# A cross-attention kernel: a new hand-written order of all engines and transfers

## The chip, the cores and the metric

The kernel runs on one core of a Trainium2 chip. The metric is the time of one execution on the device, in microseconds, and smaller is better. The time before is a median of three runs. One more execution was recorded by the profiler, and all rows of the trace come from that one.

## The reference

The layer is a cross-attention with two short sets of keys that share one set of queries. The batch is 2, a sequence has 2048 tokens of 640 channels, there are 20 heads of 32, and each set has 77 keys made from a context of 1024 channels. Everything is float32.

```python
q = split_heads(x @ Wq.T)                                   # (2, 20, 2048, 32)
k, v = split_heads(text @ Wk.T), split_heads(text @ Wv.T)   # 77 keys
k_ip, v_ip = split_heads(ip @ Wk_ip.T), split_heads(ip @ Wv_ip.T)
out = merge_heads(softmax(q k.T / sqrt(32)) v)
out += merge_heads(softmax(q k_ip.T / sqrt(32)) v_ip)
result = out @ Wo.T + bo + x
```

## The kernel before

All matrices lie with the contracted dimension first. A group of four heads fills the 128 partitions, so there are five groups of heads and two batches: ten pairs, q = 0 to 9. The tokens of a pair are taken in two halves of 1024, which gives twenty units, u = 0 to 19, and each half is two blocks of 512 tokens.

The body of the kernel is one long string, SCHEDULE. It is split into words, and `emit` turns each word into instructions. The framework adds the waits between engines that the data need, and each engine and the queue of SyncE (SP) run their own instructions strictly in the order of the string. The order of the words is therefore the order of each engine, and a word that waits holds up all later words of its engine. These are the words:

- `q.u.h@bank` (`queries`, L199): TensorE's query product of one block, ten instructions. `cq.u.h` is ScalarE's copy of it out of its bank.
- `k.c.t`, `v.c.t` (`project_kv`, L140): keys and values of a group of heads for one set, sixteen instructions each. `ck` and `cv` are their copies by ScalarE. `SQ.c` (L150) is VectorE's transposition of the values, and `VS.q.half` (`spread_v`, L156) spreads one half of them by eight small transfers of 20 KB.
- `Rs.u@half` (`scores`, L231): the scores of group s of unit u; groups 0 and 1 hold three tiles of 128 tokens (24 instructions), group 2 holds two (16). They fill four of the eight banks.
- `K` (ScalarE's copy of scores, L243), `M` (VectorE's maximum, L279 or L282), `S` (GpSimd's subtraction, L293), `E` (exponential, L299 or L267), `D` (VectorE's sum, L304), `I` (reciprocal, L309), `N` (GpSimd's normalisation, L314), `T` (VectorE's transposition, L321): the softmax of one group.
- `A.q@half` (`attend`, L330): attention of a pair, 160 instructions. `CA.q` is its copy.
- `m`, `G`, `W`, `o` and their copies `cm`, `co`: the output product of batch 0, as seven products per block (L488, L498) on sums that GpSimd makes. `p`, `z`, `F`, `V`, `X`, `Y`, `yz`: the output product of batch 1, with 33 products (L469, L846) on sums of weights (`V`) and of tokens (`X`); the last letter, `p` or `d`, says whether GpSimd or VectorE makes them. `Y` adds a product to an output and sends the output when it is complete.
- Transfers on SP: `LX.u.h` a block of tokens of batch 1 (1280 KB, `load_block`, L184), `LQ.q` query weights (320 KB, L190), `LK.n` key or value weights (512 KB, `load_w`, L130), `LO` the output weights (1600 KB, L162), `SF.i.part` residual rows (256 KB), `SS.i.part` finished rows (256 KB).

A load waits until the last reader of its buffer is done. Three buffers hold query weights, four hold key and value weights, and three hold the tokens of batch 1, in turn:

```python
def place_of(u, h):
    _, b, _, sub = step_of(u)
    return late.index((u, h)) % XROOM if b else sub * NH + h

def load_w(n):
    src, c = wlist[n]
    w = wslots[n % len(wslots)]
    nc.sync.dma_start(out=w, in_=src[:, ts(c, P)].rearrange("(k p) o -> p k o", p=P))

def load_wq(q):
    c = q % NC
    nc.sync.dma_start(
        out=wqs[q % 3], in_=WqT[:, ts(c, P)].rearrange("(k p) o -> p k o", p=P)
    )
```

So LX.10.1 waits for q.10.0, LQ.6 for q.7.1, and LX.14.1 for q.14.0.

Three sets choose the form of a group's softmax. A group in none of them takes the words K, M, S, E, D, I, N, T, with one exponential for the whole group. A group in BIASED has no S: its exponential is row by row, with the maximum as a bias. A group in DIRECT has no K either; its maximum and its exponential read the scores' banks. A group in SUMMED has no D: the exponential adds up its sums. Twenty-one groups of sixty were row by row.

Of the kernel before, what the change touches and what calls it, by code (L numbers as in the profile page):

```python
# [20 lines left out]
def kernel(  # L21
# [43 lines left out]
        (11, 0), (12, 0), (13, 0), (13, 2), (14, 0), (14, 2), (15, 1), (15, 2), (16, 2), (18, 1),  # L65
    }
    BIASED = {
        (3, 2), (4, 0), (5, 2), (6, 2), (8, 2), (9, 2), (10, 2), (11, 2), (12, 2), (18, 2), (19, 2),
    }
    SUMMED = {  # L70
        (10, 2), (12, 0), (12, 2), (13, 0), (13, 2), (14, 0), (15, 1), (16, 2), (18, 1), (18, 2), (19, 2),
# [480 lines left out]
    for t in range(2):  # L552
# [336 lines left out]
```

## Time and profile before

| | |
|---|---|
| median of three runs | 499.93 us (498.37 to 500.46) |
| the profiled execution | 503.08 us, span 501.3 us |
| mean granted clock of TensorE | 0.997 |
| TensorE (PE) busy | 492.2 us, 98% |
| VectorE (DVE), ScalarE (ACT), GpSimd (POOL) busy | 410.7, 306.8, 376.5 us |
| moved | 69.38 MB, mean 138 GB/s |
| TensorE's products | 4114 |

The span runs from the first to the last instruction of the program; the execution's time has 1.8 us more around it. In the rows, PE is TensorE's products and PEld its weight loads, which run beside the products. A row of the chain has its start in us, its length in us, and what ran. In the timelines, a bracket at the end has the idle time before the instruction and what released it. A row of the waits has the total in us, the count and the longest. A row of the groups has the busy time in us and the mean of one in ns. In the table of stretches, a row has the length, the busy time and the count of each engine, then TensorE's granted clock, the share of the DMA engines and GB/s. In the DMA view, q1 is the transfers that the kernel issues and q8 is a queue of instructions: packets, MB, and share of the engines' time.

### The profile page before, as it was taken

What the parts mean: (1) busy time and instruction counts of PE and PEld (TensorE: products, weight loads), DVE (VectorE), ACT (ScalarE), POOL (GpSimd) and SP (SyncE); (2) the same over time, 40 slices, a digit from 0 to 9 for tenths busy, and PEclk for the clock granted to TensorE, in tenths of its full rate; (3) what the DMA queues carried; (4) which work ended last, traced back from release to release, by engine and by line L of the source; (5) the groups of instructions that cost most, each with busy time, mean ns of one, the idle gap of its engine ahead of it and who ended that gap; (6) DMA issues with size and microseconds to landing.
All of it is one profiled execution on the core that took longest, in us unless ns stands there. A gap on an engine that the chain in (4) does not pass through costs nothing.

```text
span 501.3 us, 10439 instructions
## 1 busy us (share of the span) xinstructions
PE 492.2 (98%) x4114; PEld 290.7 (58%) x4114; DVE 410.7 (82%) x409; ACT 306.8 (61%) x970; POOL 376.5 (75%) x166
## 2 busy tenths in 40 slices
PE   9999999999999989999999999999999999999997
PEld 5665757567557547446646655665655685444442
DVE  0069989989999986978996888678799889998875
ACT  1175768798786866757999877485677955100000
POOL 0079998779898895968876748665889889799850
PEclk9999999999999998999999999999999999999999
DMA  8975403243044490748416337628442203320125
GB/s 264 356 209 151 133 3 100 54 119 84 23 112 150 150 288 19 248 133 330 134 54 229 94 119 274 222 87 264 144 158 90 86 1 106 127 84 1 43 101 192
DMA packets 67473, 69.38 MB, mean 138 GB/s; under 512 B 5472, under 2 KB 47200, under 8 KB 67424
## 3 DMA queue, kind: packets, MB, share of 16 engines
q1 hardware_dynamic: 66704, 68.00, 43.0%
q8 instruction: 32, 0.52, 0.4%
q10 hardware_dynamic: 720, 0.72, 0.4%
q14 instruction: 17, 0.14, 0.1%
HBM read 54.94 MB, written 10.49 MB: 131 GB/s over the span
## 4 chain that ended last, share of the span: by engine, by line
PE 90%; DMA 6%; SPq 2%; issue 1%; DVE 0%; ACT 0%
PE bank L199 30%; PE bank L846 11%; PE bank L488 10%; PE bank L231 10%; PE bank L330 10%; PE bank L140 9%; PE bank L469 7%; PE bank L498 3%; DMA x<-in_x_dram 2%; DMA aT<-in_L_xattn_Wk_ip_dram 2%; DMA wq<-in_L_xattn_Wq_dram 1%; DMA wo_ct<-in_L_xattn_Wo_dram 1%; SPq L156 1%; SPq L532 1%; SPq L130 0%
## 5 line engine op out<-in xcount | busy, mean ns | idle before, releaser
L314 POOL TENSOR_TENSOR pb<-pb,rden 128x1848 f32<-128x1848 f32 (+1 forms) x60 | 176.0, 2942 | 39.2 <-DVE rden L309 35.1
L199 PE MATMUL bank<-x,wq 128*128 128x512 f32 x400 | 180.0, 600 | 0.1
L293 POOL TENSOR_TENSOR pb<-pb,mx 128x1848 f32<-128x1848 f32 (+1 forms) x39 | 121.7, 3129 | 60.4 <-DVE mx L279 55.3
L199 PEld LDWEIGHTS bank<-x,wq 128*128 128x128 f32 x400 | 74.5, 191 | 85.9 <-issue 82.3
L321 DVE STREAM_TRANSPOSE pb<-pb 128x1920 f32<-128x1920 f32 (+1 forms) x60 | 115.8, 1934 | 6.3 <-POOL pb L314 5.9
L279 DVE TENSOR_REDUCE mx<-pb 128x24 f32<-128x1848 f32 (+1 forms) x50 | 91.4, 1843 | 31.6 <-ACT pb L243 31.5
L243 ACT COPY pb<-bank 128x462 f32<-128x462 f32 (+1 forms) x200 | 85.3, 540 | 42.2 <-PE bank L231 41.8
L304 DVE TENSOR_REDUCE den<-pb 128x24 f32<-128x1848 f32 (+1 forms) x49 | 91.5, 1878 | 15.6 <-ACT pb L299 11.9
L299 ACT ACTIVATE pb<-pb 128x1848 f32<-128x1848 f32 (+1 forms) x39 | 65.4, 1680 | 17.2 <-POOL pb L293 17.0
L267 ACT ACTIVATE pb<-bank,mx 128x77 f32<-128x77 f32 x208 | 59.1, 390 | 12.3 <-DVE mx L282 12.2
L231 PEld LDWEIGHTS bank<-kT,qT 32*128 32x128 f32 x1280 | 45.8, 184 | 29.7 <-issue 20.3
L231 PE MATMUL bank<-kT,qT 32*128 32x154 f32 x1280 | 57.0, 306 | 3.3 <-issue 2.6
L330 PE MATMUL bank<-pb,v 32*32 32x512 f32 x1600 | 55.2, 597 | 0.0
L267 ACT ACTIVATE pb<-pb,mx 128x77 f32<-128x77 f32 x184 | 52.7, 357 | 1.1 <-DVE mx L279 0.8
L140 PE MATMUL bank<-wo_ct,aT 128*128 128x154 f32 x320 | 46.9, 302 | 0.2 <-DMA aT<-in_L_xattn_Wk_ip_dram 0.2
L140 PEld LDWEIGHTS bank<-wo_ct,aT 128*128 128x128 f32 x320 | 44.4, 194 | 3.4 <-issue 2.8
L330 PEld LDWEIGHTS bank<-pb,v 32*32 32x32 f32 x1600 | 30.4, 103 | 21.7 <-issue 9.6
L267 ACT ACTIVATION_READ_ACCUMULATOR pb<-bank,mx 128x1 f32 x152 | 40.2, 273 | 0.0
L469 PE MATMUL bank<-aT,wo_ct 128*128 128x512 f32 x80 | 36.4, 596 | 0.0
L209 ACT ACTIVATE qT<-bank 128x512 f32<-128x512 f32 x40 | 24.3, 613 | 19.4 <-PE bank L199 19.3
L488 PE MATMUL bank<-aT,wo_ct 128*128 128x256 f32 x128 | 32.5, 386 | 0.6 <-DMA wo_ct<-in_L_xattn_Wo_dram 0.6
L488 PEld LDWEIGHTS bank<-aT,wo_ct 128*128 128x128 f32 x128 | 23.6, 190 | 8.3 <-issue 4.0
(75 smaller groups left out, 435.8 us busy)
## 6 DMA issues: line engine op xcount, KB each, us to landing
x<-in_x_dram SPq DMA_DIRECT2D x20, 1280.0 KB, 7.1
out_dram<-acc SPq DMA_DIRECT2D x20, 256.0 KB, 2.3
x<-in_x_dram SPq DMA_DIRECT2D x18, 256.0 KB, 5.4
acc<-in_x_dram SPq DMA_DIRECT2D x16, 256.0 KB, 3.7
out_dram<-x SPq DMA_DIRECT2D x15, 256.0 KB, 2.1
v<-vS SPq DMA_DIRECT2D x160, 20.0 KB, 2.0
wq<-in_L_xattn_Wq_dram SPq DMA_DIRECT2D x9, 320.0 KB, 4.7
aT<-in_L_xattn_Wk_dram SPq DMA_DIRECT2D x5, 512.0 KB, 5.6
```

Of the source, the lines that this page charges most:

```text
L140: nc.tensor.matmul(keys_in(out), loaded[n][:, k, :], cT[:, k, :, t, :], start=(k == 0), stop=(k == NCC - 1))
L199: nc.tensor.matmul(pq, wqs[q % 3][:, k, :], xs[place_of(u, h)][:, k, :], start=(k == 0), stop=(k == NC - 1),)
L231: nc.tensor.matmul(ps[g][:, ts(t, 2 * L)], qTs[(u, h)][g * D : (g + 1) * D, ts(st, P)], kT[g * D : (g + 1) * D, c, b].rearrange("p t l -> ...
L243: nc.scalar.copy(keys_of(u, s)[:, :, g], ps[g][:, : n * 2 * L].rearrange("p (n l) -> p n l", n=n))
L267: nc.scalar.activation(row, row if ps is None else rows_in(ps[g], n)[:, t, x], AF.Exp, bias=maxs[(u, s)][:, *one], accum_out=None if den i ...
L279: nc.vector.tensor_reduce(mx, rows_of(u, s), AX.X, ALU.max, negate=negate)
L293: nc.gpsimd.tensor_tensor(rows_of(u, s), rows_of(u, s), maxs[(u, s)].unsqueeze(3).to_broadcast([P, n, 2, L]), ALU.subtract)
L304: nc.vector.tensor_reduce(den_of(u, s), rows_of(u, s), AX.X, ALU.add)
L314: nc.gpsimd.tensor_tensor(rows_of(u, s), rows_of(u, s), rdens[(u, s)].unsqueeze(3).to_broadcast([P, n, 2, L]), ALU.mult)
L321: nc.vector.transpose(p, p)
L330: nc.tensor.matmul(pa[r][g * D : (g + 1) * D, :], v4s[q % 2][rows, g, k, :], zones[rows, :, g, k, :], start=(k == 0), stop=(k == NK - 1),)
L488: nc.tensor.matmul(part, w_of[m][:, kp, op], t_of(m, b, i)[:, kp], start=(op == kp == 0 and m in (1, 2, 5)), stop=(op == 1 and kp == 1 and ...
```

## The change

Only the three sets and the string change. The same words stand in it, except for those of seven groups whose form changes and for twenty sums V and X that change their engine, ten each way. TensorE's order is nearly the same up to A.9: a few neighbours are exchanged. Behind A.9 its products come in another order. The transfers on SP are in a new order throughout, and the words of the other engines are exchanged with neighbours in many places. Twenty groups are row by row.

```diff
     DIRECT = {
-        (11, 0), (12, 0), (13, 0), (13, 2), (14, 0), (14, 2), (15, 1), (15, 2), (16, 2), (18, 1),
+        (11, 0), (12, 0), (13, 0), (13, 2), (14, 0), (14, 2), (15, 1), (15, 2), (16, 2), (18, 1), (19, 2),
     }
     BIASED = {
-        (3, 2), (4, 0), (5, 2), (6, 2), (8, 2), (9, 2), (10, 2), (11, 2), (12, 2), (18, 2), (19, 2),
+        (3, 2), (4, 2), (5, 2), (6, 0), (8, 2), (9, 2), (10, 2), (12, 2), (18, 2),
     }
     SUMMED = {
-        (10, 2), (12, 0), (12, 2), (13, 0), (13, 2), (14, 0), (15, 1), (16, 2), (18, 1), (18, 2), (19, 2),
+        (4, 2), (10, 2), (12, 0), (12, 2), (13, 0), (13, 2), (14, 0), (15, 1), (15, 2), (16, 2), (18, 1),
+        (18, 2),
     }
```

The string, around the places that the prediction speaks of. Around A.0:

```diff
...
-        "K0.1 N1.0 T0.0 q.2.1@0 LK.5 LQ.3 K1.1 LK.7 I2.0 M0.1 LK.4 SF.0.1 N2.0 VS.0.1 T1.0 R2.1@1 S0.1 q.3.0@1 K2.1 "
-        "M1.1 T2.0 S1.1 E0.1 M2.1 v.1.0@3 D0.1 S2.1 k.1.1@6 E1.1 I0.1 cq.2.1 D1.1 k.1.0@7 N0.1 E2.1 ck.1.1 cq.3.0 "
...
+        "R1.1@1 K0.1 N1.0 I2.0 q.2.1@0 T0.0 K1.1 M0.1 N2.0 T1.0 R2.1@1 S0.1 v.1.0@2 K2.1 M1.1 k.1.1@7 LK.10 T2.0 "
+        "S1.1 E0.1 k.1.0@6 M2.1 cq.2.1 D0.1 q.3.0@3 S2.1 E1.1 LK.8 SQ.0 VS.0.1 I0.1 ck.1.0 cv.1.0 D1.1 ck.1.1 N0.1 "
+        "E2.1 I1.1 D2.1 R2.2@1 cq.3.0 R0.2@0 K2.2 N1.1 T0.1 q.3.1@5 K0.2 LQ.3 LK.7 I2.1 VS.0.0 M2.2 N2.1 M0.2 "
...
```

Around A.2 and A.3:

```diff
...
-        "q.8.0@0 I2.5 T0.5 N2.5 K0.6 VS.2.1 I1.5 T2.5 N1.5 M0.6 R1.6@1 v.3.0@2 K1.6 M2.6 S0.6 LK.15 SF.0.3 E2.6 "
-        "M1.6 q.7.1@3 LK.16 T1.5 S1.6 E0.6 D2.6 A.2@1 I2.6 cv.3.0 D0.6 cq.7.1 N2.6 E1.6 I0.6 cq.8.0 T2.6 N0.6 D1.6 "
...
-        "N1.7 T0.7 E2.8 M0.8 R1.8@1 LX.11.0 q.10.0@1 LQ.7 LK.18 T1.7 K1.8 S0.8 cq.9.1 M1.8 E0.8 A.3@1 LX.10.1 D2.8 "
-        "S1.8 cq.10.0 D0.8 I0.8 E1.8 I2.8 N0.8 R0.9@0 VS.5.0 CA.3 D1.8 v.4.0@4 N2.8 K0.9 T0.8 v.4.1@5 cv.4.0 I1.8 "
-        "T2.8 N1.8 R2.9@0 cv.4.1 SQ.4 R1.9@1 K2.9 VS.4.0 M0.9 q.11.1@0 K1.9 M2.9 S0.9 M1.9 E2.9 LQ.6 q.11.0@1 T1.8 "
...
+        "q.7.1@1 T1.5 S1.6 D2.6 A.2@1 LQ.6 LK.17 I2.6 LX.10.0 E1.6 N2.6 D0.6 cv.3.0 cq.8.0 I0.6 cq.7.1 D1.6 N0.6 "
...
+        "N2.7 cq.8.1 D1.7 ck.4.0 R2.8@0 cq.9.0 N0.7 R0.8@1 K2.8 T2.7 q.9.1@0 K0.8 LK.18 M2.8 VS.3.1 I1.7 E2.8 T0.7 "
+        "N1.7 M0.8 R1.8@1 q.10.0@2 K1.8 LX.11.0 T1.7 S0.8 M1.8 E0.8 A.3@1 LX.10.1 D2.8 S1.8 cq.9.1 D0.8 cq.10.0 "
+        "I0.8 E1.8 I2.8 N0.8 R0.9@0 CA.3 D1.8 v.4.0@4 N2.8 K0.9 T0.8 v.4.1@5 cv.4.0 T2.8 R2.9@0 cv.4.1 I1.8 R1.9@1 "
+        "M0.9 K2.9 N1.8 q.11.1@0 K1.9 M2.9 SQ.4 E2.9 S0.9 VS.4.0 M1.9 q.11.0@4 T1.8 S1.9 E0.9 D2.9 LX.12.0 VS.4.1 "
...
```

Around A.4, A.5 and A.7:

```diff
...
-        "cq.10.1 I1.9 T2.9 R2.10@0 K0.10 N1.9 q.12.0@4 T0.9 K2.10 VS.5.1 T1.9 R1.10@0 cq.12.0 M0.10 A.4@1 K1.10 LO "
...
-        "M1.12 A.5@0 LX.14.1 N0.12 SF.1.4 LX.15.1 VS.6.1 S1.12 T0.12 m2.1@4 cm6.0 CA.5 I2.12 N2.12 E1.12 R0.13@0 "
...
-        "q.17.1@4 T1.15 K0.16 M0.16 R2.16@0 LX.19.0 VS.8.0 m1.2@6 S0.16 M2.16 E2.16 M1.16 q.18.0@5 S1.16 E0.16 "
-        "I2.16 A.7@0 LX.18.1 N2.16 E1.16 D0.16 cq.17.1 D1.16 G6.2 I1.16 I0.16 m5.2@7 N1.16 T2.16 VS.9.1 CA.7 cm1.2 "
...
+        "N1.9 q.12.0@4 SF.0.4 LX.12.1 K2.10 LO VS.5.0 T1.9 R1.10@0 cq.12.0 M0.10 A.4@1 K1.10 S0.10 M1.10 M2.10 "
...
+        "LQ.7 o.0@1 LX.13.0 LX.14.0 LX.13.1 D1.10 W1 cm2.0 R1.11@1 co.0 I1.10 R2.11@0 D0.11 K1.11 N1.10 m1.0@4 "
...
+        "E1.11 R2.12@0 cm1.0 m3.0 SS.0.0 K2.12 S2.11 T2.10 LX.16.0 D1.11 SF.1.0 R0.12@0 G6.0 E2.11 VS.6.0 q.13.1@7 "
+        "cq.13.0 I1.11 M0.12 N1.11 E0.12 D2.11 I2.11 q.14.0@5 T1.11 N2.11 SS.0.4 T2.11 SF.1.4 I0.12 A.5@0 LX.14.1 "
...
+        "R2.16@0 LX.19.0 S1.16 SS.1.3 m1.2@7 M2.16 SF.2.1 E2.16 SF.2.2 M0.16 q.18.0@5 G6.2 S0.16 E1.16 I2.16 A.7@0 "
+        "SF.2.3 cq.17.1 D1.16 LX.18.1 N2.16 E0.16 I1.16 N1.16 T2.16 D0.16 m5.2@4 VS.9.0 CA.7 I0.16 cm1.2 cm5.2 "
...
```

101 rows, old and new, of the table SCHEDULE are left out of this document.

## The prediction

> **What bounds the kernel now.** I began with the page's busy times, went on to the chain that ended last, and then asked the DMA view and the timelines about the few places where that chain is not TensorE.
>
> ```profile
> span 501.3 us, 10439 instructions
> PE 492.2 (98%) x4114; PEld 290.7 (58%) x4114; DVE 410.7 (82%) x409; ACT 306.8 (61%) x970; POOL 376.5 (75%) x166
> q8 instruction: 32, 0.52, 0.4%
> ...
> 112.73 4.41 PE bank L140 x32
> ...
> 143.37 5.45 PE bank L330 x151
> 148.82 1.00 PE bank L231 x24
> ...
> 178.35 5.45 PE bank L330 x154
> 183.81 0.85 PE bank L231 x17
> 184.66 2.38 issue
> ...
> 187.62 5.99 PE bank L140 x32
> ...
> 269.12 0.85 PE bank L231 x17
> ...
> 270.70 1.93 PE bank L488 x8
> ...
> 448.55 48.99 PE bank L846 x114
> ```
>
> TensorE (PE) is busy for 98% of the span, and its last 114 products run without a gap. So only what interrupts PE, and what new interruptions are added, can move the end. The words of TensorE are the same ones in both schedules: 231 words, with 46 runs of score words, 14 of them doubled. Its own work costs the same before and after, and no gain can be larger than its gaps.
>
> The largest gap follows attention A.3. A full group of 24 score instructions takes 1.00 us (148.82); here 17 of them run, then PE stands for 2.38 us on "issue", which means that no engine or transfer of data released it. The group, with the 7 left over, lasts from 183.81 to 187.62, 3.81 us, so 2.81 us are lost. The two key and value projections behind it take 5.99 us against 4.41 us at 112.73, another 1.58 us. The stretches show why:
>
> ```profile
> 186.00:188.00 2.00, 0.97 (x9) 0.76 (x9) 2.00 (x2) 0.69 (x3) 2.00 (x1) 0.85 0.38 109
> 188.00:190.00 2.00, 2.00 (x9) 2.00 (x9) 1.61 (x3) 1.24 (x3) 1.63 (x2) 0.50 0.15 31
> ```
>
> The third figure from the right is the granted clock: 0.85 from 186 to 188 and 0.50 from 188 to 190. The gap itself costs 2.81 us and the halved clock behind it 1.58 us, together 4.39 us. The Trainium skill ("TensorE: Matmul & The Clock Gate", What's actually happening) has the clock halve after at least one idle window of about 3.4 us. The trace halves it after 2.38 us of idling, so the measurement decides; by the page alone only the 2.81 us would be at stake here.
>
> What PE waited for is its own code. The page has 32 instruction packets of 0.52 MB in all; 4114 products and 4114 weight loads are 8228 instructions, so a packet holds some 257 of them. Where do they arrive? These are windows of 0.2 us at A.3 and at A.2, then the SyncE queue (SP) around A.3, and the DMA view of 180 to 184:
>
> ```profile
> q8 instruction: 1, 0.02, 34.3%
> ...
> q8 instruction: 1, 0.02, 36.9%
> ...
> 174.57 0.53 SPq L184 DMA_DIRECT2D x<-in_x_dram  x1
> 175.20 0.47 SPq L190 DMA_DIRECT2D wq<-in_L_xattn_Wq_dram  x1
> 175.72 0.52 SPq L130 DMA_DIRECT2D aT<-in_L_xattn_Wv_dram  x1
> 178.39 0.98 SPq L184 DMA_DIRECT2D x<-in_x_dram  x1
> ...
> q1 hardware_dynamic: 1893, 1.31, 114.5%
> ```
>
> The first row is 184.3 to 184.5: the code packet starts then, 6 us after A.3 began, and PE goes on at 187.04 (184.66 + 2.38), 2.6 us later. At A.2 (145.4 to 145.6) it starts 2.1 us after attention began, with no other traffic in the window, and PE never stops. The last row is 180 to 184: 1.31 MB, 0.33 MB per us, with the engines full and no code packet. The loads LX.11.0, LQ.7, LK.18 and LX.10.1 put 3.4 MB in its way.
>
> **The change part by part.** First what goes.
>
> A.3: LQ.7 moves to m2.0, LK.18 ahead of VS.3.1, and LX.11.0 is left alone between VS.3.1 and A.3. If the code arrives in time this returns 4.39 us. The same at A.5, where LX.14.1, SF.1.4 and LX.15.1 are issued together: the group from 269.12 to 270.70 takes 1.58 us instead of 1.00. After the change only LX.14.1 stands there, and 0.58 us returns.
>
> ```profile
> PE bank L488 <- DMA wo_ct<-in_L_xattn_Wo_dram: 0.6, 1, 0.6
> PE bank L231 <- ACT kT L684: 0.4, 1, 0.4
> 50.93 6.34 PE bank L140 x48
> 69.19 5.45 PE bank L330 x150
> 139.08 4.29 PE bank L199 x10
> ```
>
> LO is moved ahead of the 16 small transfers of VS.5.0 and VS.5.1, so m2.0 no longer waits 0.6 us for it. q.3.0 is moved between k.1.0 and R2.2, which gives the copy of k.1.0 the 4.29 us of a query product (139.08) and removes the 0.4 us. What goes is 4.39 + 0.58 + 0.6 + 0.4 = 5.97 us.
>
> Now what comes. Each item is between nothing and the end that I name.
>
> ```profile
> 352.91 5.46 PE bank L330 x154
> 353.22 0.59 SPq L184 DMA_DIRECT2D x<-in_x_dram  x1
> 36.64 5.89 SPq L156 DMA_DIRECT2D v<-vS  x8
> v<-vS SPq DMA_DIRECT2D x160, 20.0 KB, 2.0
> 193.96 0.57 DVE L150 STREAM_TRANSPOSE vS<-vT 128x160 f32<-128x160 f32 x2 [4.35 <-ACT vT L686]
> 196.64 6.55 POOL L293 TENSOR_TENSOR pb<-pb,mx 128x1848 f32<-128x1848 f32 x2 [4.97 <-ACT pb L243]
> 212.76 2.18 DVE L321 STREAM_TRANSPOSE pb<-pb 128x1920 f32<-128x1920 f32 x1 [0.72 <-POOL pb L314]
> 215.30 5.52 PE L330 MATMUL bank<-pb,v 32*32 32x512 f32 x160
> x<-in_x_dram SPq DMA_DIRECT2D x1, 1280.0 KB, 6.4
> 209.81 4.56 PE L199 MATMUL bank<-x,wq 128*128 128x512 f32 x10
> L279 DVE TENSOR_REDUCE mx<-pb 128x24 f32<-128x1848 f32 (+1 forms) x50 | 91.4, 1843 | 31.6 <-ACT pb L243 31.5
> ```
>
> A.2: LQ.6 (320 KB) now waits for the end of q.7.1, 143.37, and is issued as A.2 starts, with LK.17 (512 KB) and LX.10.0 (1280 KB) behind it. The code packet of A.2 starts at 145.5. Counting 257 instructions back three times from the stop at A.3 puts the same point for A.2 at 149.1, inside the scores of 148.82; with 2.6 us from packet to use there is 1.0 us to spare. LQ.6 alone is 1.0 us of transfer, LQ.6 and LK.17 2.5 us, so 0 to 1.5 us, and I take 0.5, nearer to LQ.6, the only one issued two microseconds ahead of the packet. A.3: LX.10.1 is still freed by q.10.0 and issued at A.3's start; its 1280 KB are 3.9 us. In the trace of before the 2.1 MB ahead of it, on their way from about 176 (an estimate, 1.5 us after the issue), end near 182.4 at that rate, and the code starts at 184.4, so 2.0 of the 3.9 us stood before the code. Alone, from about 180, that gives 182 for the packet and 184.6 for PE, which stops at 184.66: 0 to 0.8, I take 0.3. A.7: LX.18.1 was issued at 353.22, behind eight VS transfers, and after A.7's start at 352.91; now only stores and fetches are ahead of it and it can come up to 1 us sooner; 0 to 1.5, I take 0.5.
>
> A.0: SQ.0 and the spread of V move from 36.64 to behind LK.8, and LK.8 waits for k.1.0. The three projections that end at 57.27 will end 4.29 us sooner, at 53.0, because q.3.0 no longer stands ahead of them. From there 0.6 for LK.8, two halves of V at 5.9, about 1.0 for LQ.3 and LK.7 between them, and 2.0 to land make 68.4, against A.0 at 68.8 (69.19 less the 0.4): nothing in the sum, 0.3 at the most.
>
> A.4: here the old stall was a cover. While PE stood, POOL idled for 4.97 us and DVE for 4.35 us. Without it POOL has 4.97 - 4.39 = 0.6 us left, and the change puts I1.8 behind the transpose T2.8 (two thirds of the 2.18 us of a full one, 1.5), so N1.8 and all POOL work behind it come 0.9 us later. T1.9 ended at 214.94, 0.36 us ahead of A.4 at 215.30. A.4 now waits 0 to 0.9 us; I take 0.6.
>
> q.12.0: it ran at 209.81, and its tokens, LX.12.0, landed at 206.4 (issued at 200.0, 6.4 to land), 3.4 us to spare. LX.12.0 follows VS.4.0, which follows SQ.4, and SQ.4 now goes behind two maxima, 1.84 and two thirds of that, 3.1 us; LQ.6 no longer stands ahead of the load, 0.6 back. That leaves 0.9 us; a landing of 7.1, the median on the page, leaves 0.2. So 0 to 0.7, and I take 0.3.
>
> The seven groups whose softmax changes form (21 to 20 row by row), the swaps on ACT, DVE and POOL, and the moved V, X and Y words cost nothing in the sum: seven V and three X words go each way between DVE and POOL, and ACT is idle 39% of the span. Without that cover one row-by-row group against one whole activation is:
>
> ```profile
> L299 ACT ACTIVATE pb<-pb 128x1848 f32<-128x1848 f32 (+1 forms) x39 | 65.4, 1680 | 17.2 <-POOL pb L293 17.0
> L267 ACT ACTIVATE pb<-pb,mx 128x77 f32<-128x77 f32 x184 | 52.7, 357 | 1.1 <-DVE mx L279 0.8
> ```
>
> 24 times 0.357 less 1.68, 6.9 us, and that once at most.
>
> What comes is 0.5 + 0.3 + 0.5 + 0.6 + 0.3 = 2.2 us, with ends 0 and 5.7. The net is 5.97 - 2.2 = 3.8 us. The profiled execution took 503.08 us, 1.8 beyond its span, so it would take 499.3. The median of the three runs, 499.93, lies 3.15 us under it. If that distance has nothing to do with the stalls, the median becomes 496.1. If it is the stalls, because code comes sooner when nothing is recorded, only 0.65 us is left to win and it stops at 499.3. The three times spread from 498.37 to 500.46, 2.1 us, a little more than one halved clock (1.58), so I think that the stalls are there in differing size, and take 2.7 of the 3.8: 497.2 us.
>
> **The rivals.** *The stalls stay.* The order of loads may have nothing to do with the late code. Then only LO and the copy of k.1.0 pay, 1.0 us, less the 0.3 of q.12.0: 499.2 us. For it: the trace shows the late packet and the traffic together only at A.3 and A.5. Against it: at A.2 the packet found no traffic and came on time. The Trainium skill speaks for this rival: "DMA: Bandwidth & Descriptors", Queues, rings and completion order, says that each DMA engine takes turns between the queues that have work, a packet at a time. By that a code packet should not wait behind 3.4 MB of another queue, and moving loads would change nothing. The trace speaks against it, with 180 to 184 all in q1.
>
> *The stall moves, and part of it is given back.* At A.2 the code goes behind LQ.6 and LK.17: 1.5 us and a halved clock, 1.58. The gain of 2.7 shrinks by 2.6 (3.1 less the 0.5 counted): 499.8 us.
>
> *Slower: code behind LX.10.0 too.* All three loads at A.2 are 2.1 MB, 6.4 us at 0.33 MB per us. With half of LX.10.0 ahead, as LX.10.1 was, the packet starts 4.4 us late; less the 1.0 to spare that is 3.4, with the clock 5.0 us, and LX.10.1 does at A.3 its 0.8 with another 1.58. Against the forecast that adds 4.5 + 2.1 = 6.6: 503.8 us. It decides from the point where LX.10.0 is queued ahead of the code, so at some time before 145.5. For it: nothing on SP stands between LK.17 and LX.10.0. Against it: its issue comes 1.2 us after A.2's start.
>
> **How the numbers follow.** Forecast 0.51, the stalls stay 0.16, the stall moves 0.14, slower 0.19. A measurement of this kernel tells about 0.5%, 2.5 us, from no change, so faster means below 497.4 and slower above 502.4. The forecast's own range is 495.0 to 499.3, with the bounds of the new waits; I put 0.43 of its 0.51 below 497.4, since the low bounds of the new waits and the full 3.8 lie there, and 0.08 within. The two middle rivals are within, 0.30, and of the slower one 0.17 is beyond 502.4 and 0.02 within. The range from 495.2 to 501.8 leaves the slower case out and little else.
>
> **What would show it.** Right: at A.3 17 and 7 score instructions become 24 in one row of 1.00 us, no "issue" of 2 us stands in the waits of PE, the granted clock is 1.00 in every stretch from 184 to 192, and m2.0 has no wait for wo_ct. Wrong: "issue" gaps behind A.2 or A.7, a clock of 0.50 there, or PE waits for T1.9 at A.4 or for x at q.12.0 of over 1 us. The forecast is wrong if PE has waits on DVE, ACT or POOL of 3 us or more in all, which the trace of before doesn't have anywhere.

## The result and the profile after

The changed kernel took 500.19 us (median of 22 runs, 499.31 to 503.24) against 499.29 for the kernel before on the same chip (22 runs, 498.10 to 502.95). The ratio is 1.001, with a 95% interval from 0.9995 to 1.0025: no change that can be measured. The prediction was 497.2 us, with 499.3 for the recorded execution; that took 503.24 us, 1.8 beyond its span, against 503.08 before. The line numbers of the code are one higher than before.

The page, its busy times and the code packets:

```profile
span 501.4 us, 10438 instructions
PE 492.5 (98%) x4114; PEld 289.9 (58%) x4114; DVE 410.4 (82%) x411; ACT 303.2 (60%) x967; POOL 377.0 (75%) x167
q8 instruction: 32, 0.52, 0.5%
```

The chain of work that ended last (start, us, what), at A.1, A.3, m2.0, A.5 and A.7:

```profile
112.29 0.98 PE bank L232 x21
113.27 0.52 issue
113.80 0.53 PE bank L232 x3
...
180.09 5.45 PE bank L331 x149
185.54 0.73 PE bank L232 x16
186.28 1.65 issue
187.93 0.54 PE bank L232 x8
188.47 6.07 PE bank L141 x32
...
227.24 1.06 PE bank L489 x4
...
269.27 1.05 PE bank L232 x24
...
352.67 5.72 PE bank L331 x154
```

The stop behind A.3 is still there: 16 score products, 1.65 us on "issue", then 8, and the two projections still take 6.07 us instead of 4.41. A new one stands behind A.1: 21 products, 0.52 us on "issue", then 3. From 112.29 to the end of the row at 114.33 is 2.04 us where a whole row takes 1.00, so 1.04 us are lost. The stop at A.5 is gone (24 products in one row of 1.05 us), and so is the wait of m2.0 for the output weights (no piece stands ahead of 227.24 in the chain). The stretches of time, with the granted clock as the third figure from the right, say the same of A.3:

```profile
186.00:188.00 2.00, 0.35 (x15) 0.23 (x9) 2.00 (x2) 1.54 (x6) 2.00 (x2) 1.00 0.04 8
188.00:190.00 2.00, 2.00 (x15) 1.84 (x15) 2.00 (x2) 1.62 (x4) 1.51 (x1) 0.66 0.04 8
```

What held the code? First the DMA view (packets, MB, share of the 16 engines) of 182.1 to 185.3, then that of 185.2 to 185.4:

```profile
q1 hardware_dynamic: 586, 1.18, 103.2%
...
q8 instruction: 1, 0.02, 31.7%
```

And SP's queue at A.3:

```profile
171.47 5.02 SPq L157 DMA_DIRECT2D v<-vS  x8
176.59 3.90 SPq L185 DMA_DIRECT2D x<-in_x_dram  x2
```

The code packet starts at about 185.3, 5.3 us after A.3 (6.1 before). In the 3.2 us from 182.1 on, when a packet that nothing holds would come, q1 moves 1.18 MB and nothing else moves. The last row is LX.11.0 at 176.59, behind the spread VS.3.1, and LX.10.1 at 180.12, just behind A.3's start. In the trace of before LX.11.0 left at 174.57, and the prediction's sum took LX.10.1 to be alone from about 180.

This recording is also 0.77 us late from the first scores on (24.32, against 23.55 in that of before). Among the waits of TensorE from 0 to 30 us it has one that before has not:

```profile
PE bank L200 <- DMA x<-in_x_dram: 0.5, 1, 0.5
```

This wait belongs to the very first query products, ahead of the first word of the string. Over the recorded executions of all kernels here the first scores begin between 22.96 and 24.32, from 23.10 to 23.96 in the old order and over the whole range in the new, and up to 28 us SP issues the same transfers in both. So it is most likely scatter of the start. But the wait for x stands in six of the ten records of the new order and in none of the eight of the old, and why is open.

### The profile page after: what moved, and what is told of

It reads as the page before. It is cut to its first block, busy times and chain, and to the rows that moved or that the text cites. A ratio compares the mean times of both kernels' runs of the same rounds, so it can differ in the third digit from the quotient of the medians.

```text
span 501.4 us, 10438 instructions
## 1 busy us (share of the span) xinstructions
PE 492.5 (98%) x4114; PEld 289.9 (58%) x4114; DVE 410.4 (82%) x411; ACT 303.2 (60%) x967; POOL 377.0 (75%) x167
## 4 chain that ended last, share of the span: by engine, by line
PE 94%; DMA 3%; SPq 1%; issue 1%; ACT 0%; DVE 0%
PE bank L200 32%; PE bank L847 11%; PE bank L331 11%; PE bank L232 11%; PE bank L489 10%; PE bank L141 9%; PE bank L470 7%; PE bank L499 3%; DMA aT<-in_L_xattn_Wk_ip_dram 2%; DMA wq<-in_L_xattn_Wq_dram 2%; SPq L533 1%; SPq L131 0%; DVE x L793 0%; ACT pb L244 0%; ACT kT L558 0%
## 5 line engine op out<-in xcount | busy, mean ns | idle before, releaser
L294 POOL TENSOR_TENSOR pb<-pb,mx 128x1848 f32<-128x1848 f32 (+1 forms) x40 | 124.0, 3108 | 57.3 <-DVE mx L280 57.0
L244 ACT COPY pb<-bank 128x462 f32<-128x462 f32 (+1 forms) x196 | 83.9, 543 | 32.4 <-PE bank L232 31.9
L305 DVE TENSOR_REDUCE den<-pb 128x24 f32<-128x1848 f32 (+1 forms) x48 | 90.1, 1883 | 14.0 <-ACT pb L300 13.8
L300 ACT ACTIVATE pb<-pb 128x1848 f32<-128x1848 f32 (+1 forms) x40 | 67.0, 1675 | 24.6 <-POOL pb L294 24.5
L268 ACT ACTIVATE pb<-bank,mx 128x77 f32<-128x77 f32 x224 | 64.0, 384 | 12.0 <-DVE mx L283 12.0
L268 ACT ACTIVATE pb<-pb,mx 128x77 f32<-128x77 f32 x152 | 44.7, 389 | 1.1 <-DVE mx L280 1.1
L268 ACT ACTIVATION_READ_ACCUMULATOR pb<-bank,mx 128x1 f32 x168 | 43.6, 265 | 0.0
```

Source lines behind the costliest of these rows:

```text
L244: nc.scalar.copy(keys_of(u, s)[:, :, g], ps[g][:, : n * 2 * L].rearrange("p (n l) -> p n l", n=n))
L268: nc.scalar.activation(row, row if ps is None else rows_in(ps[g], n)[:, t, x], AF.Exp, bias=maxs[(u, s)][:, *one], accum_out=None if den i ...
L294: nc.gpsimd.tensor_tensor(rows_of(u, s), rows_of(u, s), maxs[(u, s)].unsqueeze(3).to_broadcast([P, n, 2, L]), ALU.subtract)
L305: nc.vector.tensor_reduce(den_of(u, s), rows_of(u, s), AX.X, ALU.add)
```

## The experiments

All words below are words of SCHEDULE; "before" and "after" name the kernel that was edited. The four kernels of one group (e1 to e4, e5 to e8, and so on) shared a chip and its runs of the kernel before. A median is one of 12 runs, for e12 and e15 of 8, for e3 of 6; "code after A.3" is the time from A.3's start to the packet's, in the recorded execution.

| run | edits | median us | before on that chip | ratio and 95% interval | stop at A.3, us | code after A.3, us |
|---|---|---|---|---|---|---|
| e1 | before, LX.10.1 later | 498.70 | 500.11 | 0.9971 [0.9951, 0.9991] | 0.3 | 4.2 |
| e2 | before, all four loads of A.3 moved | 497.72 | 500.11 | 0.9943 [0.9924, 0.9962] | none | 2.0 |
| e3 | before, LX.11.0 twice | 507.21 | 500.11 | 1.0125 [1.0088, 1.0162] | none | 2.1 |
| e4 | after, A.1, A.3 and A.7 cleared | 498.64 | 500.11 | 0.9966 [0.9947, 0.9986] | none | 2.2 |
| e5 | before, LQ.7 and LK.18 moved | 499.98 | 500.83 | 0.9974 [0.9951, 0.9998] | 1.5 | 5.3 |
| e6 | after, LQ.5 later | 500.10 | 500.83 | 0.9982 [0.9960, 1.0004] | 1.6 | 5.2 |
| e7 | after, A.3 cleared | 499.20 | 500.83 | 0.9971 [0.9948, 0.9994] | none | 2.2 |
| e8 | e2 and the change's k.1.0 | 498.97 | 500.83 | 0.9970 [0.9948, 0.9992] | none | 2.2 |
| e9 | after, LX.10.1 later (VS.5.0 ahead of it) | 498.75 | 500.54 | 0.9964 [0.9947, 0.9981] | none | 2.3 |
| e10 | after, LX.11.0 and LK.18 sooner | 501.50 | 500.54 | 1.0024 [1.0003, 1.0045] | 1.7 | 5.6 |
| e11 | after, as it is | 500.38 | 500.54 | 0.9994 [0.9976, 1.0013] | 1.1 | 4.9 |
| e12 | e2 again | 497.70 | 500.54 | 0.9931 [0.9906, 0.9957] | none | 2.2 |
| e13 | e9 and e6 | 498.74 | 499.61 | 0.9965 [0.9942, 0.9987] | none | 2.1 |
| e14 | e13 with SQ.4 sooner | 498.68 | 499.61 | 0.9982 [0.9967, 0.9998] | none | 2.1 |
| e15 | e2 with two loads at A.1 | 497.40 | 499.61 | 0.9957 [0.9938, 0.9976] | none | 2.2 |
| e16 | e9 again | 499.22 | 499.61 | 0.9995 [0.9980, 1.0010] | none | 2.3 |

The median of the kernel before lies between 499.3 and 500.8 from chip to chip, so a difference of less than 1 us is read only between kernels of one group. Within one chip, much of the spread is the halved clock: in the runs of before on the chip of e9 to e12, 9 of 31 have a mean granted clock of 0.997 or less and a median of 502.0, and the other 22 one of 500.0. (One halved stretch like that at A.3 makes the mean 0.997.) It does not explain the difference between chips, since the medians of the other runs still lie from 499.3 to 500.3. Of the changed kernel's 22 runs, two have it. Over all groups, 32 of 126 runs of before have it, and 13 of the 70 runs of the kernels that leave LX.10.1 at A.3 (after, e5, e6, e10, e11); of the 124 runs of those that move it, none.

### Does traffic hold the code at all? e1, e2

```diff
-M1.8 E0.8 A.3@1 LX.10.1 D2.8
+M1.8 E0.8 A.3@1 D2.8
-R0.9@0 VS.5.0 CA.3
+R0.9@0 VS.5.0 LX.10.1 CA.3
```

> The kernel before, with one transfer moved: LX.10.1 goes behind VS.5.0 on SP, so it leaves only after A.3. Queue theory (a code packet waits for the loads queued ahead of it): 2.1 MB are still ahead of the code of A.3, so its packet starts near 182.4 instead of 184.4; the stop of 2.38 us behind A.3 becomes 0 to 0.5 us, the clock stays at 1.00 there, and the recorded span falls by about 4 us. Rival (the code is late for a reason of its own, such as its place in the program): the stop and the halved clock stay, span as before. For the timed runs: if they have the same stop, the median falls by 1 to 4 us against before; if the stop belongs to recorded executions only, no change.

For e2 besides, LK.18 behind LK.19, LX.11.0 behind LX.11.1, LQ.7 behind m2.0:

```diff
-R1.8@1 LX.11.0 q.10.0@1 LQ.7 LK.18 T1.7
+R1.8@1 q.10.0@1 T1.7
```

> The kernel before, with everything cleared from the way of A.3's code: LK.18 goes behind LK.19, LX.11.0 behind LX.11.1, LX.10.1 behind VS.5.0, LQ.7 behind m2.0. Queue theory: the packet starts about 2.1 us after A.3 as it does at A.2, no stop, clock 1.00, span 4.4 us shorter. Rival (own reason): unchanged. Timed: if runs of before differ among themselves by whether this stop occurs (they range from 498.1 to 502), this kernel's runs lie together at 498 to 499 and the median is about 1 us below before; if not, they spread as before does.

The chain at A.3, first that of e1:

```profile
184.22 0.85 PE bank L231 x17
185.34 0.54 PE bank L231 x7
185.88 4.41 PE bank L140 x32
```

and that of e2:

```profile
184.01 1.00 PE bank L231 x24
```

With one load moved, the stop shrinks from 2.38 to 0.3 us (185.34 less the end of the row before, 185.07), and the projections have the full clock again. The packet still comes 4.2 us after A.3, 2 us later than in e2, so the three loads that are left hold it too. With four moved, the row of 24 is whole. The medians fall by 1.4 and 2.4 us. So late code behind loads is real, in timed runs too, and moving loads does change the time, which the rival that the stalls stay denied. The gain of 2.4 us is nearly the 2.7 that the change was predicted to bring.

### A dose that missed: e3

```diff
-LX.11.0 q.10.0@1
+LX.11.0 LY.11.0 q.10.0@1
```

LY.11.0 loads the same block into the same buffer once more.

> The kernel before, with LX.11.0 issued twice in a row, the same 1280 KB into the same buffer: 3.9 us more traffic ahead of the code of A.3. Queue theory: the packet starts 3 to 4 us later, at 187 to 188.5, PE stops for 5 to 6.5 us behind A.3, the clock is halved, and the span grows by 3 to 4 us. Rival (own reason): span within 1 us of before. Timed: if the queue acts in timed runs as it does in recorded ones, the median grows by 3 to 6 us, since the stop then occurs in every run; if it acts only when recorded, by less than 1 us.

It did something else. The second load had to wait for the first, since both write one buffer, and held up SP, so that the code found an empty queue and came on time. What came late were the weights LK.18. SP's queue, where one row of 6.64 us holds both loads of the block:

```profile
173.61 6.64 SPq L184 DMA_DIRECT2D x<-in_x_dram  x2
```

the waits of TensorE:

```profile
PE bank L140 <- DMA aT<-in_L_xattn_Wv_dram: 5.2, 1, 5.2
```

and two of the stretches, with the granted clock at 0.50:

```profile
188.00:190.00 2.00, 0.49 (x2) 0.52 (x3) 1.17 (x1) 0.00 (x0) 2.00 (x1) 0.50 1.02 363
...
192.00:194.00 2.00, 2.00 (x9) 2.00 (x9) 0.00 (x0) 0.01 (x1) 0.00 (x0) 0.50 0.14 36
```

This says nothing about the dose. It does show what 5.2 us of waiting cost: about 7 us in the median, because the clock is halved besides, at 0.50 in all three stretches from 188 to 194 and in part of the two beside them.

### What was it in the changed kernel? e4, e6, e7

All of e4's edits, with those of e6 and e7 among them:

```diff
-A.1@1 LQ.5 LK.11 cq.5.1            (e4, e6: LQ.5 behind VS.2.1)
+A.1@1 LK.11 cq.5.1
-K0.8 LK.18 M2.8                    (e4, e7: LK.18 behind LK.19)
+K0.8 M2.8
-K1.8 LX.11.0 T1.7                  (e4, e7: LX.11.0 behind VS.3.0)
+K1.8 T1.7
-A.3@1 LX.10.1 D2.8                 (e4, e7: behind VS.5.0, which goes behind CA.3)
+A.3@1 D2.8
-D1.16 LX.18.1 N2.16                (e4 alone: LX.18.1 behind VS.9.0; LK.12, LQ.4 behind ck.2.0)
+D1.16 N2.16
```

> The changed kernel, with loads moved away from the three places where its code still came late: LQ.4 and LK.12 ahead of VS.1.0 and LQ.5 behind VS.2.1 (A.1); LK.18 behind LK.19, LX.11.0 behind VS.3.0, VS.5.0 behind CA.3 and LX.10.1 behind VS.5.0 (A.3); LX.18.1 behind VS.9.0 (A.7). Queue theory: no stop at A.1, A.3 or A.7 and a clock of 1.00; the span falls from 501.4 by about 0.9 + 1.65 + 1.7 + 0.3 = 4.5 us to 497, and the timed median to 497.5 to 499, 1 to 2 us below the changed kernel's. Rival (own reason, or a floor that the new order itself raised): the median stays at 500.2.

> The changed kernel with LQ.5 moved behind VS.2.1, so that only LK.11 stands near the code packet of A.1. Theory: the 0.5 us stop in the scores behind A.1 goes, A.3 keeps its stop of 1.6 to 2.4 us with the halved clock behind it, and the median falls by 0.4 to 0.6 us to about 499.7. Rival (the timed runs do not have that stop, it belongs to the recorded execution): the row of 24 is whole, but the median stays at 500.2 within 0.2.

> The changed kernel with the neighbourhood of A.3 cleared (LK.18 behind LK.19, LX.11.0 behind VS.3.0, VS.5.0 behind CA.3, LX.10.1 behind VS.5.0), and A.1 and A.7 left alone. Theory: the packet starts 2 us after A.3 instead of 5.3, the 1.65 us stop and the halved clock behind it go, the profiled execution falls by 2.9 us or more, and the median by 1.0 to 1.7 us (the timed runs have the stop but seldom the halved clock) to 498.5 to 499.2. Rival (in timed runs the stop is not there): the median stays at 500.0 to 500.4.

Clearing all of it brings 498.64 us, clearing A.3 alone 499.20, and A.1 alone 500.10, the first on another chip than the other two. For e4 and e7 that is about what the theory had, for e6 it decides nothing: its record has no stop at A.1, though its row still takes 1.28 us instead of 1.00, and its interval against before overlaps that of the unchanged order of after. The timed effect of A.1 is taken up further down.

### Which load at A.3? e5, e9, e10, e11, e12

e5 is the change's own part at A.3 in the old order:

```diff
-LX.11.1 R2.8@0
+LX.11.1 LK.18 R2.8@0
-q.10.0@1 LQ.7 LK.18 T1.7
+q.10.0@1 T1.7
-m2.0@2 M0.11
+m2.0@2 LQ.7 M0.11
```

> The kernel before with the change's own edits at A.3 and nothing else: LQ.7 behind m2.0, LK.18 behind LX.11.1; LX.11.0 and LX.10.1 stay where they are. Theory (the code packet waits for the loads queued ahead, and the change failed at A.3 because LX.11.0 left late there): here LX.11.0 still leaves at about 174.6, its 1280 KB are through by 180, and the packet waits only for part of LX.10.1: it starts at 182 to 182.7, PE stops 0 to 0.4 us, the granted clock stays 1.00 from 184 to 192, and the median is within 0.3 us of the run that moved LX.10.1 alone, 498.4 to 499.0. Rival (it is LX.10.1, issued as the attention starts, that holds the packet, wherever LX.11.0 stands): the packet starts at 184 or later, PE stops 1.5 us or more, the clock is halved, and the median stays at 500.1.

The rival was right, though the packet came at 183.5 and not at 184 or later. The chain:

```profile
184.52 1.52 issue
186.04 0.78 PE bank L231 x7
186.82 5.79 PE bank L140 x32
```

and the DMA view of 180.2 to 183.5:

```profile
q1 hardware_dynamic: 664, 1.33, 105.0%
```

LX.11.0 left at 175.7 here, before LX.10.1 at 178.25, and 0.83 MB of other loads were out of the way, yet the code came 5.3 us after A.3, 0.8 sooner than in the kernel before. From the time at which it would come unheld it waited for 1.33 MB; in the kernel before, from 180.4 to 184.4, q1 moved the same 1.3 MB (331 GB/s for 4.0 us), only slower. With LX.10.1 there, what stood ahead of it did not matter much. My theory for the change's miss, that LX.11.0 left too late, was wrong.

The pair that decides it takes the one or the other from the changed kernel. In e9 LX.10.1 goes behind CA.3, with VS.5.0 put ahead of it there; in e10 LX.11.0 and LK.18 leave sooner:

```diff
e9:
-A.3@1 LX.10.1 D2.8
+A.3@1 D2.8
-CA.3 D1.8
+CA.3 VS.5.0 LX.10.1 D1.8
-LO VS.5.0 T1.9
+LO T1.9
e10:
-VS.3.0 I2.7
+VS.3.0 LX.11.0 I2.7
-K1.8 LX.11.0 T1.7
+K1.8 T1.7
-K0.8 LK.18 M2.8                    (LK.18 behind LK.19)
+K0.8 M2.8
```

> The changed kernel with LX.10.1 alone taken from A.3 (VS.5.0 behind CA.3 and LX.10.1 behind VS.5.0); LX.11.0, LK.18 and all of A.1 stay. Theory (LX.10.1, issued in the tenth of a microsecond behind A.3's start, goes ahead of the code request that comes 2 us after A.3, and holds it by its whole 1280 KB): without it the packet waits only for the rest of LX.11.0 and starts 2.0 to 3.2 us after A.3 instead of 5.3; no stop of 0.5 us or more at A.3, clock 1.00, and 1.0 to 1.7 us off the median of the changed kernel. Rival (LX.11.0, which left 2 us later than the prediction had it, is what holds the packet): it starts 4 us or more after A.3, the stop stays at 1 us or more.

> The changed kernel with LX.11.0 behind VS.3.0 and LK.18 behind LK.19, so that both are gone well before A.3; LX.10.1 stays at A.3. Theory: LX.10.1 alone does it, the packet starts 4.7 to 5.4 us after A.3, PE stops 1.0 to 1.8 us in the scores behind it, and the median moves by less than 0.5 us. Rival (the step of the prediction: half of LX.10.1 goes behind the code, and LX.11.0's late issue was the fault): the packet starts 3.7 us or less after A.3, no stop over 0.3 us, and the median falls by 1 us or more.

> The changed kernel as it is, on the chip of the other three of this call, as the measure for them. All theories: packet of A.3 5.2 to 5.4 us after A.3, a stop of 1.5 to 2.4 us there and of about 0.5 us at A.1, median within 0.2% of the kernel before.

> The kernel of the run e2 (before, with all four loads at A.3 moved), on the chip of the changed kernel. Theory: packet 2 us after A.3, no stop, and a median 2 to 2.8 us under the kernel before, and as far under the changed kernel. Rival (the 0.57% of that run belonged to that chip): within 1.2 us of before.

The chain at A.3, of e9:

```profile
184.44 1.00 PE bank L232 x24
```

of e10:

```profile
185.83 1.71 issue
187.54 0.54 PE bank L232 x8
188.09 6.06 PE bank L141 x32
```

and of e11:

```profile
186.17 1.10 issue
187.27 0.55 PE bank L232 x8
187.81 4.41 PE bank L141 x32
```

In e10, SP's queue:

```profile
170.52 0.53 SPq L185 DMA_DIRECT2D x<-in_x_dram  x1
...
179.67 0.37 SPq L185 DMA_DIRECT2D x<-in_x_dram  x1
```

and the DMA view of 181.6 to 185.1:

```profile
q1 hardware_dynamic: 573, 1.16, 96.2%
```

With LX.10.1 gone from A.3 the stop is gone, though LX.11.0 and LK.18 stay. With LX.10.1 alone left, nine microseconds behind the load ahead of it, the code comes 5.6 us after A.3 and the stop is 1.71 us with the halved clock. All recordings bear this out: in the six with LX.10.1 at A.3 and nothing that delays it (before, after, e5, e6, e10, e11) the code comes 4.9 to 6.1 us after A.3 and TensorE stops for 1.1 us or more; in the eleven that move it the stop is 0.3 us in e1 and nothing in the others. On this one chip the changed kernel takes 500.38 us, without LX.10.1 at A.3 498.75, and with LX.11.0 moved instead 501.50. So one word that the change left where it was kept 1.6 us of the gain back. That e10 is 1.1 us longer than the changed kernel, where less than 0.5 was expected, goes with the halved clock: six of its twelve runs have it, and one of e11's.

e12 confirms the old order with its four loads moved, 497.70 us, 2.7 us under the changed kernel on the same chip.

e11 shows one thing more: a stop of 1.10 us here left the clock whole (4.41 us for the projections), while 1.52 us in e5 and 1.65 in the first recording were followed by a halved one.

### What remains in the changed kernel? e13 to e16

Two of the expectations below say that q.12.0 waits for its tokens by 0.5 to 1 us. That was a misreading: the row of waits it was taken from belongs to the first products of the kernel, as the view from 0 to 30 us above shows, and TensorE does not wait at q.12.0 in the kernel after.

```diff
e13: the edits of e9, and
-A.1@1 LQ.5 LK.11 cq.5.1
+A.1@1 LK.11 cq.5.1                 (LQ.5 behind VS.2.1)
e14: those of e13, and
-cv.4.1 I1.8
+cv.4.1 SQ.4 I1.8
-M2.9 SQ.4 E2.9 S0.9 VS.4.0 M1.9    (VS.4.0 behind K2.9)
+M2.9 E2.9 S0.9 M1.9
e15: those of e2, and
-M1.4 LQ.5 A.1@1 S1.4              (LK.11 stood behind LK.10)
+M1.4 A.1@1 LQ.5 LK.11 S1.4
```

> The changed kernel with LX.10.1 moved as in e9 and, besides, LQ.5 behind VS.2.1, so that the code of A.1 has only LK.11 near it. Theory (the stop behind A.1 is what is left over): the 21 and 3 products there become one row of 24, 1.04 us come off the record from A.1 to R2.5, and the median is 0.7 to 1.1 us under the run with LX.10.1 alone (e16 in this call). Rival (the timed runs have no stop at A.1): within 0.3 us of it.

> e13 with SQ.4 behind cv.4.1 and VS.4.0 behind K2.9, about where the kernel before has them. Theory: LX.12.0 leaves 2 to 3 us sooner, the wait of q.12.0 for x (0.5 us with the stop of A.3, 1.0 us without it) goes, and the median is 0.5 to 1.0 us under e13, at the cleared kernel before. Rival (the wait only becomes one for the maxima or for another load): within 0.3 us of e13.

> The kernel before with A.3 cleared (e2) and LQ.5 and LK.11 issued as A.1 starts, as the change has them. Theory: the code packet of A.1 starts 4 us or more after A.1 instead of 2.1, PE stops 0.3 to 0.7 us in the scores behind it, the piece from A.1 to R2.5 takes 11.5 to 12.0 us instead of 10.86, and the median is 0.7 to 1.1 us over that of e2, near 498.6. Rival (other orders at A.1, not these two loads, make the stop): the packet comes at 2.1 and the median is e2's 497.7.

> The kernel of e9 again, as the measure for the other three on their chip. All theories: packet of A.3 at 2.0 to 2.6 us after it, a stop of about 0.5 us or less at A.1, q.12.0 waits about 1 us, and 0.2 to 0.5% under the kernel before.

The chain at A.1, of e16:

```profile
112.70 0.51 issue
113.20 0.53 PE bank L232 x3
```

and of e13:

```profile
111.36 0.98 PE bank L232 x21
112.35 0.53 PE bank L232 x3
```

e13 takes the "issue" piece of 0.5 us away but not the split row, and its median is 0.48 us under that of e16; the two intervals just overlap. So the new stop at A.1 most likely costs about half a microsecond in timed runs too, half of what was expected. It is not in every execution: e9, whose string is that of e16, has the whole row at A.1, with the code 3.1 us after A.1 instead of 4.5:

```profile
112.22 1.00 PE bank L232 x24
```

e16 missed what was expected of it: 0.2 to 0.5% under the kernel before, where the ratio came out at 0.9995, with an interval on both sides of 1. On its chip only 3 of the 31 runs of before have the halved clock, and there is less to win against it; the 1.6 us of e9 are against the changed kernel, which did not run on this chip.

The waits of TensorE in e14:

```profile
PE bank L331 <- ACT pb L244: 0.6, 1, 0.6
```

Its rival held, for more than one reason: there was no wait at q.12.0 to take away, and this wait of A.4, for ScalarE's copy of scores, came up in the record.

e15 did not make the stop: its row of 24 at A.1 takes 1.00 us. SP's queue:

```profile
104.17 0.37 SPq L190 DMA_DIRECT2D wq<-in_L_xattn_Wq_dram  x1
```

Though they stand behind the word A.1, its two loads still left two microseconds before attention, because q.5.1, whose buffer LQ.5 needs, ends there before a value projection that stands ahead of A.1. In the changed kernel that order is turned round: v.2.0 comes first, q.5.1 is the last word ahead of A.1, and LQ.5 leaves as A.1 begins. So the stop at A.1 comes from the order of TensorE's words together with the loads, not from the place of the loads alone. That this order is the cause is read from the two traces, and no run turned it round.

Three runs of the cleared old order (e2, e12, e15) stand at 497.4 to 497.7 us, and the best changed ones at 498.6 to 498.8. About 1.3 us between e15 and e13 on one chip are left. In their records 0.5 us of it lies behind A.1 (11.38 against 10.86 us from A.1 to R2.5) and 1.05 at A.7 and the stage behind it. At A.7 the code packet and LX.18.1 overlap, and attention there took from 5.45 us up to 5.95 in the recordings of the old order (e12) and 6.59 in those of the new (e10). That part was not settled.

### The change's k.1.0 alone: e8

```diff
-S0.1 q.3.0@1 K2.1
+S0.1 K2.1
-k.1.0@7 N0.1
+k.1.0@7 q.3.0@1 N0.1
-ck.1.1 cq.3.0 D2.1                 (cq.3.0 behind ck.1.0)
+ck.1.1 D2.1
```

> The kernel before with all of A.3's loads cleared, as in the run e2, and the change's edit on k.1.0: q.3.0 behind k.1.0, with ck.1.0 ahead of cq.3.0. Theory: no issue stop, and the 0.4 us wait of R2.2 for kT goes, so 0.3 to 0.5 us under that run: 497.3. Rival (the wait only moves, to the copy of another product or to A.0): 497.7 or more.

```profile
PE bank L140 <- DMA aT<-in_L_xattn_Wk_dram: 0.9, 1, 0.9
```

The 0.4 us wait for the copy went, and 0.9 us of waiting for weights took its place, because k.1.0 now ran 4.3 us sooner while its load did not. The changed kernel has no such wait; it issues LK.5 and LK.4 at the start. So in the record this one edit, taken alone, gains nothing. In timed runs that is not shown: the ratio of 0.9970 is above the 0.9943 and 0.9931 of e2 and e12, which ran on other chips, but its interval overlaps theirs.

## Why the prediction was wrong

**The step that failed is the forecast for A.3.** It let 4.39 us return and allowed 0.3 us for LX.10.1, which it took to let the packet through by 182. In the records, the way from A.3 to the projections behind the stop went from 178.35 to 187.62 before, 9.27 us, and from 180.09 to 188.47 after, 8.38: 0.89 us returned, and the halved clock stayed. The sum had taken from the trace of before that about half of LX.10.1 was served behind the code, and had started that load at "about 180" without the rest. e10 shows that alone it holds the code as long as the whole crowd did: 5.6 us after A.3. The bytes that pass between the unheld time and the packet are 1.33 MB in e5, 1.18 MB after and 1.16 MB in e10, about one LX load (1280 KB), whatever stood ahead of it. That LX.11.0 would be through by 180 was wrong too (it left at 176.59), but e10 shows that it did not matter. Why the load held the packet whole here, when half of it seemed to pass behind the packet in the trace of before, is open.

**The median was sized from the wrong base.** Between 0.65 us (the stalls are not in the median) and 3.8 (all of it) the prediction took 2.7. The runs show that the halved clock, 1.58 us of the sum, is in the median of neither kernel: of before's runs 3 to 11 in some 30 have it, by chip, and of the changed kernel's 2 in 22. Taking away the stop was worth 1.6 us from e11 to e9 and 2.4 to 2.8 us from before to e2 and e12. So of the 2.7 us that were forecast LX.10.1 explains 1.6; about half a microsecond more is most likely A.1, and the rest was not placed.

**What was not in the sum.** The stop behind A.1: 1.04 us in the record, about 0.5 in timed runs. The prediction looked at the loads around A.2, A.3, A.5 and A.7 and not at LQ.5 and LK.11, which leave as A.1 starts:

```profile
106.87 0.37 SPq L191 DMA_DIRECT2D wq<-in_L_xattn_Wq_dram  x1
```

**What was right, by the record.** LO: the wait of 0.6 is gone, and none of the ten recordings of the new order has it. The copy of k.1.0: its wait of 0.4 is not among the waits any more. A.7: 5.72 us for attention, 0.26 more, within the predicted 0 to 1.5. A.0: no wait.

**What came out as predicted by luck.** A.5: 0.58 predicted, 1.58 less 1.05 measured. But the stop there stands in the one recording of before alone. All seven edits of the old order (e1, e2, e3, e5, e8, e12, e15) leave the loads at A.5 as they were and have a whole row of 24; here that of e2:

```profile
264.20 1.00 PE bank L231 x24
```

So the 0.58 us were most likely a piece of one execution, and no run shows that the change's edit at A.5 took them away.

**What did not happen.** A.4 does not wait for T1.9, but the stop that covered it is still there; e14, without the stop, shows a wait of 0.6 us at A.4. That is the size predicted, but the wait is for ScalarE's copy (L244) and not for T1.9, and e9 and e16, without the stop too, show none. q.12.0 does not wait. And A.2, the place of two rivals, has no stop. SP's queue there:

```profile
145.01 0.37 SPq L191 DMA_DIRECT2D wq<-in_L_xattn_Wq_dram  x1
146.00 0.58 SPq L185 DMA_DIRECT2D x<-in_x_dram  x1
```

and in the DMA view of 146.8 to 147.0:

```profile
q8 instruction: 1, 0.02, 47.1%
```

The packet came 2 us after attention began, with all three loads issued ahead of it, and was not held. In e9 and e10, with the same three loads issued there, it came 3.1 us after, and still without a stop.

So the record's account is: 0.9 (A.3), 0.5 (A.5), 0.6 (LO) and 0.4 (k.1.0) gained, 2.4 in all; 1.04 (A.1), 0.77 (the later start) and 0.26 (A.7) lost, 2.1. That leaves 0.3 us of gain, where the record shows 0.16 of loss; the other half microsecond is spread over the stages and was not placed.

Of the rivals, none came as written. The nearest is the one that the stalls stay, 499.2 us, but by luck, since its reason is wrong: traffic does hold the code, and the change left the load that does it. The Trainium skill's rule behind that rival ("DMA: Bandwidth & Descriptors", Queues, rings and completion order), that the DMA engines take turns between queues, would soon let through a packet that is asked for. In e10 it came only after 1.16 MB of q1 had passed, and in e9, without that load, 2.3 us after A.3. So the measurement decides against what the rival made of the rule, that moving loads changes nothing. Whether the turns themselves fail is not shown, since no trace shows when the packet was asked for.

## What to carry to other kernels

When TensorE shows "issue" gaps, find the code packets in the DMA view and the large load that is issued a microsecond or two before each would come; moving that one load can do more than thinning the queue ahead of it, as at A.3, though not every such load does harm, as A.2 shows. Before pricing a stop, see whether a second recording has it: the one at A.5 was in one of eight recordings of the old order. Before crediting a reordering with a stall's return, list every load that will still be issued there, and where each is released: a load's place in the queue's order matters less than the word whose end sets it free. And weigh a halved clock in one recording by how many timed runs have it.

## What the runs showed of the hardware that was not expected

- **A short stop can halve the clock, but its length alone does not decide.** Stops at A.3 of 1.52 us (e5), 1.65 (after) and 1.71 (e10) were followed by a granted clock near 0.50 and projections of 5.79 to 6.07 us; a stop of 1.10 us (e11) was not, with 4.41 us. But in e1 TensorE waits 1.70 us for the output weights, from 222.99 to 224.69, and the clock stays at 1.00 (its wait, then two stretches):

```profile
PE bank L488 <- DMA wo_ct<-in_L_xattn_Wo_dram: 1.7, 1, 1.7
222.00:224.00 2.00, 0.99 (x24) 0.76 (x24) 0.92 (x2) 1.94 (x4) 2.00 (x1) 1.00 1.04 413
224.00:226.00 2.00, 1.31 (x6) 1.18 (x7) 2.00 (x4) 2.00 (x11) 1.87 (x2) 1.00 1.07 390
```

  The Trainium skill ("TensorE: Matmul & The Clock Gate", What's actually happening) gives an idle window of about 3.4 us for that; at A.3 half of it was enough, and in e1 half of it was not. What tells the two apart is open.
- **A code packet behind a load waits for about one whole load.** It was held for 3.2 to 4.0 us, while 1.16 to 1.33 MB passed, in four recordings (before, after, e5, e10), where LX.10.1 was issued a tenth of a microsecond behind A.3's start, with 0 to 2.1 MB issued ahead of that load in the microseconds before. Without LX.10.1 but with the 2.1 MB (e1) it was held for about 2 us. What stays open is why, in the kernel before, the packet went ahead of the rest of the queue, and why LQ.6, LK.17 and LX.10.0, issued as early before A.2's packet, did not hold it in the recording of after, and held it by about 1 us only in e9 and e10. A race between the first bytes of a load and the request for the packet might do it, but no run tested it.
